# Graph attention on one core: attention and feed-forward woven by clocks, four gather buffers, adjacency lists in quarter rows

## The chip, the cores and the metric

One NeuronCore of one Trainium2 chip runs the whole kernel in one launch. Its engines are TensorE (PE), VectorE (DVE), ScalarE (ACT), GpSimd (POOL) and SyncE (SP). The time is device microseconds of the launch. DMAs are issued from SP, ACT and POOL; the indirect ones, which gather or scatter rows by an index list, from POOL alone.

## The reference

Inputs are `x` and `h_target` (4096 x 512, float32), an adjacency matrix `adj` (4096 x 4096, int32, about 0.4% ones: both directions of a random mask of density 0.00195, and the diagonal), a node mask of ones, and the weights of one transformer layer with eight heads of 64.

```python
hs, ht = layer_norm(x), layer_norm(h_target)
q, k, v = (ht @ Wq + bq) / 8, hs @ Wk + bk, hs @ Wv + bv
logits  = where(adj != 0, q . k, -1e30)          # per head, 4096 x 4096
ctx     = softmax(logits) @ v
ht      = layer_norm(ht + ctx @ Wo + bo)
out     = layer_norm(x + ht + gelu(ht @ W1) @ W2)   # W1: 512 x 2048
```

## The kernel before

Since a row of `adj` has some 8 to 40 ones, the kernel doesn't build the 4096 x 4096 logits. For every target row it makes a list of its neighbours, sorts rows by the length of the list, and for each tile of 128 rows gathers neighbour rows of keys and values, one neighbour ("slot") per row at a time. A tile runs as many slots as its longest row has neighbours; these caps are constants (`CAPS_A`, `CAPS_B`, 600 slots in all over 32 tiles). A general path stands behind a flag and isn't taken.

Stage one. `source_group` normalises 512 rows of `x` and writes their keys and values to a table `kvd` in DRAM (one row of 1024 floats per node). `target_group` does the same for queries, with the residual beside them, into the tables `tqd` (part 0 for the first 20 tiles of rows, part 1 for the other 12). `edges(i)` makes the lists of 128 rows: it loads the adjacency row by halves (2048 columns), ACT takes the sign and counts, DVE multiplies by column numbers within segments of 128 and takes the 8 largest of every segment (`max`), and then five rounds of `max` and `match_replace` merge 256 candidates into 40. Part 0's lists run beside all eight source groups and five target groups. `sort(0)` ranks the 20 tiles' rows by list length and scatters their records with 20 indirect DMAs.

Stage two: the remaining three target groups, nine of the 36 list steps of part 1, and the attention of pair 0.

Stage three. Tiles are handled in pairs; the caps are paired so that pairs hold 35 to 38 slots, but for pair 0 (23), pair 1 (53) and pair 10 (50). `attend(i)` takes four slots at a time: four gathers from POOL into one buffer `kv` (pool `kp`, L734), DVE multiplies the keys by the q row (L781) and reduces per head (L784), ACT takes exp (L787), DVE multiplies the values by it (L768), and PE adds the values up by transposing them into one PSUM tile (L772). A batch's values are done behind the next batch's keys. At the end of a tile the sums are inverted, spread by transposes, and Wo is applied (L814); the addition that gives `h` (L816) is followed by `front(i + 2)`, which requests a later tile's q rows. At the end of a pair, `h` is normalised (POOL's power L584, ACT L834), transposed (PE L843) and becomes `h2T`. `feed(g)` is the feed-forward of a pair: hidden layer (L864), gelu (L867), output layer (L874), last normalisation, and an indirect DMA to the output (L907).

The order is written by weaving generators. `_weave` before takes streams with a number of steps and always advances the one that has done the smallest share of its steps; it is called once per pair, with that pair's attention, the feed-forward of the pair before, and up to eight list steps (three make one tile of lists; so part 1's lists end beside pair 4, and `sort(1)` follows them). The framework takes this order as a priority; its scheduler places instructions on each engine's queue, allocates buffers and writes all waits. On the chip every queue runs in its order.

When stage two is over, its pools are closed and W1 and W2 are loaded into their place.

Of the kernel before, what the change touches and what calls it, by code (L numbers as in the profile page):

```python
# [8 lines left out]
F32 = mybir.dt.float32  # L9
I32 = mybir.dt.int32  # L10
# [382 lines left out]
def _weave(*streams):  # L393

    live = [[g, n, 0] for g, n in streams]
    while live:
        s = min(live, key=lambda s: s[2] / s[1])
        s[2] += 1
        if next(s[0], StopIteration) is StopIteration:
            live.remove(s)  # L400


def _take(gen, n):

    for _ in range(n):
        if next(gen, StopIteration) is StopIteration:
            return
        yield
# [3 lines left out]
def adj_resnorm_kernel(  # L412
# [43 lines left out]
    HW = N // 2  # L456
    SEG = N // P
    SH = SEG // 2
# [28 lines left out]
    with tc.tile_pool(name="keep", bufs=1) as keep:  # L487
# [14 lines left out]
        with ExitStack() as late:  # L502
            lp = late.enter_context(tc.tile_pool(name="lists", bufs=1))
            kp = late.enter_context(tc.tile_pool(name="kv", bufs=3))
# [12 lines left out]
            for i, v in enumerate((ln1_scale, ln1_bias, ln2_scale, ln2_bias, bv)):  # L517
# [6 lines left out]
            dpart = lp.tile([P, NT, 2], F32, name="dpart")  # L524
            cnt = lp.tile([P, NT], F32, name="cnt")
            segoff = lp.tile([P, SEG, 8], F32, name="segoff")
            iota_i = lp.tile([P, SEG, 8], I32, name="iota_i")
            nc.gpsimd.iota(iota_i, pattern=[[P, SEG], [0, 8]], base=0, channel_multiplier=0)
            nc.vector.tensor_copy(segoff, iota_i)
            lio = lp.tile([P, P], BF16, name="lio")  # L530
            nc.gpsimd.iota(iota_i.rearrange("p s e -> p (s e)")[:, :P], pattern=[[1, P]], base=1,
                           channel_multiplier=0)
            nc.vector.tensor_copy(lio, iota_i.rearrange("p s e -> p (s e)")[:, :P])
# [60 lines left out]
            def edges(i):  # L594

                cand = lp.tile([P, SEG, 8], F32, name="cand", bufs=2)
                for h in range(2):
                    a = lp.tile([P, HW], I32, name="a", bufs=2)
                    nc.sync.dma_start(a, adj[i * P:(i + 1) * P, h * HW:(h + 1) * HW])
# [3 lines left out]
                    nc.vector.tensor_tensor(sg, sg, lio.unsqueeze(1).to_broadcast([P, SH, P]),  # L603
                                            ALU.mult)
                    for s in range(SH):
                        nc.vector.max(cand[:, h * SH + s, :], sg[:, s, :])  # L606
                    yield
                gid = lp.tile([P, SEG, 8], F32, name="gid")
                nc.vector.scalar_tensor_tensor(gid, cand, 0.0, segoff, op0=ALU.is_gt, op1=ALU.mult)
# [10 lines left out]
                yield  # L620
# [5 lines left out]
            def sort(part):  # L626
# [13 lines left out]
                oh = pool.tile([P, SH, P], BF16, name="sg", bufs=2)  # L640
# [4 lines left out]
                pos = pool.tile([P, HW], I32, name="a", bufs=2).bitcast(F32)  # L645
# [20 lines left out]
                for i in range(n):  # L666
                    ins = nc.gpsimd.indirect_dma_start(
                        out=recs_d[part][:, :],
                        out_offset=bass.IndirectOffsetOnAxis(ap=ranki[:, i:i + 1], axis=0),
                        in_=R[:, i0 + i, :], in_offset=None)  # L670

                    tc.declare_no_dep(ins.ins, group=f"scatter{part}", reason="other rows")
                    tc.add_to_no_dep_group(f"scatter{part}", ins.ins)

# [22 lines left out]
            def source_group(g, t=None):  # L697
                _, hT = normed(x, g, t)
                yield
                for j in range(G):  # L700
                    kvr = ip.tile([P, 2 * D], F32, name="row")
                    for half, w in enumerate((wk, wv)):
                        pkv = psi.tile([P, D], F32, name="pq")
                        for kc in range(KC):
                            nc.tensor.matmul(pkv, hT[:, kc, j * P:(j + 1) * P], w[:, kc, :],  # L705
                                             start=kc == 0, stop=kc == KC - 1)
                        nc.scalar.copy(kvr[:, half * D:(half + 1) * D], pkv)  # L707
                    r0 = 1 + (g * G + j) * P
                    nc.scalar.dma_start(kvd[r0:r0 + P, :], kvr)
                    yield  # L710

            def target_group(g):
                t, hT = normed(h_target, g)
                yield
                for j in range(G):
# [12 lines left out]
                    yield  # L728


            recs, tqs = {}, {}
# [6 lines left out]
            def prefetch(i):  # L738
# [3 lines left out]
                part = 1 if r0 >= PARTS[1][0] * P else 0  # L742
                r0 -= PARTS[part][0] * P
# [12 lines left out]
            def attend(i):  # L756

                rec, tq, cap = recs[i], tqs[i], TILES[i][1]
                nc.vector.tensor_copy(degs[:, i:i + 1], rec[:, MAXE:MAXE + 1])
                has = sp.tile([P, MAXE], F32, name="has", bufs=1)  # L760
                nc.vector.tensor_scalar(has[:, :cap], rec[:, :cap], 0.0, None, op0=ALU.is_gt)
# [14 lines left out]
                for j0 in range(0, cap, S):  # L776
# [14 lines left out]
                    yield  # L791
                values(*pend.pop(0))
                pm = sp.tile([P, MAXE, H], F32, name="pm", bufs=1)
# [17 lines left out]
                yield  # L811
# [5 lines left out]
                yield h  # L817

            def attend_group(g, res):
                mv = sp.tile([P, T2, 2], F32, name="mv2")  # L820
                hs = []
                for j in range(T2):
                    i = g * T2 + j
                    if i + 3 not in recs:
                        prefetch(i + 3)
                    for r in attend(i):
                        if r is not None:
                            hs.append(r)
                            front(i + 2)
                            stats(sp, r, mv[:, j, :], "n2")  # L830
                        yield
# [4 lines left out]
                yield  # L836
# [12 lines left out]
                res.append(h2T)  # L849

            def att_steps(g):
                return sum(-(-TILES[g * T2 + j][1] // S) + 2 for j in range(T2)) + 2


            def feed(g, h2T):
# [22 lines left out]
                yield  # L878
                for f2 in range(1, FC // 2):
                    now = hidden(f2)  # L880
                    yield
# [15 lines left out]
                    yield  # L897
# [14 lines left out]
            FEED = FC + 1  # L912


            ed = all_edges()
            NA, NBT = PARTS[0][1], PARTS[1][1]
            first = 3 * NA
            work = [source_group(0, first_x)]
            for _ in range(2):
                next(work[0])  # L920
# [3 lines left out]
            order = work + src[:2]  # L924
# [3 lines left out]
            per = 5  # L928
            def chain(gens):
                for g in gens:  # L930
                    yield from g
            _weave((chain(order), per * len(order) - 2), (_take(ed, first), first))
# [3 lines left out]
            for i in range(2):  # L936
                front(i)
            res = []
            qb = chain([target_group(g) for g in range(NA // G, NG)])
            left = 3 * NBT  # L940
            w0 = 9
            _weave((qb, per * (NG - NA // G)), (attend_group(0, res), att_steps(0)),
                   (_take(ed, w0), w0))
            left -= w0
# [10 lines left out]
            for g in range(1, NT // T2):  # L955
                before = res.pop()
                streams = [(attend_group(g, res), att_steps(g)), (feed(g - 1, before), FEED)]
                if left > 0:
                    n = min(left, 8)
                    streams.append((_take(ed, n), n))  # L960
                    left -= n
                    if left == 0:
                        def end_lists(g0=streams.pop()[0]):
                            yield from g0
                            sort(1)
                        streams.append((end_lists(), n))
                _weave(*streams)
            for _ in feed(NT // T2 - 1, res.pop()):
                pass
# [57 lines left out]
```

## Time and profile before

| | |
|---|---|
| median of 3 runs | 2280.63 us (2275.54 to 2283.97) |
| the profiled execution | 2282.18 us, its span 2280.3 us, mean granted clock of TensorE 0.899 |
| busy, us and share of the span | PE 1832.5 (80%), DVE 1670.0 (73%), POOL 1119.4 (49%), ACT 706.2 (31%) |
| gathers of key/value rows | 600 on POOL, 775.1 us busy |
| DMA | 482.28 MB, mean 211 GB/s |

The span is the time from the first to the last instruction; the rest of the execution's time lies around it. Matmuls are pipelined, and their ends are modelled, so PE's busy share is no measure of a peak. The granted clock is a share of 2.4 GHz. POOL's spans are rough. A wait is put down to the releaser that came last.

### The profile page before, as it was taken

To read this page: it belongs to the slowest core of one execution; us is meant where nothing else is said; L and a number is where in the kernel's file an instruction comes from. 1 tells how busy PE (TensorE), PEld (TensorE's weight loads), DVE (VectorE), ACT (ScalarE), POOL (GpSimd) and SP (SyncE) were. 2 spreads that over 40 slices of the span, in tenths; PEclk is the share of its full clock that TensorE was granted. 3 is DMA by queue.
4 is the path that set the end of the run, shared out by engine and by line. 5 is a ranking of instruction groups with operands and counts; after the bars stand their busy time and mean duration, and the time that the engine had idled before them with its cause. 6 is when DMAs were issued, how large, how long until landed. Compare 5 with 4: busy or idle time off the path is not lost. (4 is left out here: it accounts for less than half of the span.)

```text
span 2280.3 us, 20645 instructions
## 1 busy us (share of the span) xinstructions
PE 1832.5 (80%) x7154; PEld 1187.8 (52%) x7154; DVE 1670.0 (73%) x2898; ACT 706.2 (31%) x962; POOL 1119.4 (49%) x887
## 2 busy tenths in 40 slices
PE   6988888457866877686779797978878898878897
PEld 3444434234544555454547565556646566655564
DVE  6998895678788888977476766768686777757540
ACT  4554453202313332231213222323313332322220
POOL 0022222777546463555555546655656556554510
PEclk9999999767877999797989898989999999989898
DMA  8766653668767566565466566666666666655520
GB/s 315 247 238 235 225 207 138 245 228 325 277 215 279 196 226 223 169 238 176 150 215 207 182 240 198 229 212 211 227 229 231 206 229 226 232 165 197 194 65 11
DMA packets 135947, 482.28 MB, mean 211 GB/s; under 512 B 19044, under 2 KB 19608, under 8 KB 127640
## 3 DMA queue, kind: packets, MB, share of 16 engines
q0 software_dynamic: 101760, 365.74, 46.9%
q1 hardware_dynamic: 28368, 96.24, 12.4%
q10 hardware_dynamic: 5704, 18.89, 2.1%
q8 instruction: 58, 0.95, 0.2%
q14 instruction: 57, 0.47, 0.1%
HBM read 438.07 MB, written 42.73 MB: 211 GB/s over the span
## 5 line engine op out<-in xcount | busy, mean ns | idle before, releaser
L734 POOL DMA_INDIRECT kv<-kvd,rec x600 | 775.1, 1292 | 535.6 <-PE cps L772 294.3
L781 DVE TENSOR_TENSOR kv<-kv,tq 128x2048 f32<-128x2048 f32 (+3 forms) x160 | 345.6, 2162 | 340.8 <-DMA kv<-kvd,rec 325.5
L772 PE MATMUL cps<-ident,kv 128*128 128x128 f32 x2400 | 344.4, 303 | 212.8 <-DVE kv L768 212.8
L864 PE MATMUL pf<-h2T,w 128*128 128x256 f32 x2048 | 494.2, 394 | 10.6 <-DMA w<-in_L_gnn_W_dram 5.7
L874 PE MATMUL po<-w,gt 128*128 128x512 f32 x1024 | 469.7, 598 | 4.8 <-ACT gt L867 4.8
L772 PEld LDWEIGHTS cps<-ident,kv 128*128 128x128 f32 x2400 | 313.0, 158 | 283.9 <-DVE kv L768 250.6
L864 PEld LDWEIGHTS pf<-h2T,w 128*128 128x128 f32 x2048 | 396.8, 199 | 99.2 <-issue 36.9
L768 DVE TENSOR_TENSOR kv<-kv,p 128x2048 f32<-128x2048 f32 (+3 forms) x160 | 343.5, 2153 | 27.1 <-ACT p L787 27.0
L784 DVE TENSOR_REDUCE lg<-kv 128x32 f32<-128x2048 f32 (+3 forms) x160 | 342.5, 2143 | 1.2
L874 PEld LDWEIGHTS po<-w,gt 128*128 128x128 f32 x1024 | 191.0, 193 | 190.0 <-issue 181.3
L787 ACT ACTIVATE p<-lg 128x32 f32<-128x32 f32 (+3 forms) x160 | 36.4, 227 | 671.5 <-DVE lg L784 671.0
L606 DVE MAX8 cand<-sg 128x8 f32<-128x128 bf16 x1024 | 227.5, 277 | 0.3
L867 ACT ACT_TABLE_LOAD x97 | 124.5, 1283 | 218.9 <-PE pf L864 218.1
L584 POOL TENSOR_TENSOR n_rs<-n_ve,mhalf 128x2 f32<-128x2 f32 (+1 forms) x48 | 50.2, 1046 | 268.9 <-DVE n_ve L583 263.1
L601 ACT ACTIVATE sg<-a 128x2048 bf16<-128x2048 int32 x64 | 122.1, 1908 | 144.5 <-DVE cand L606 110.4
L814 PE MATMUL m<-wo,ct 128*128 128x512 f32 x256 | 133.9, 672 | 31.4 <-DVE ct L810 31.2
L718 PE MATMUL pq<-wq,hT 128*128 128x512 f32 x256 | 125.8, 641 | 15.0 <-DVE row L721 15.0
L787 ACT ACT_TABLE_LOAD x96 | 123.2, 1283 | 1.7
L867 ACT ACTIVATE gt<-pf 128x512 f32<-128x512 f32 x128 | 76.1, 597 | 152.0 <-PE pf L864 151.0
L705 PE MATMUL pq<-wk,hT 128*128 128x512 f32 x256 | 120.8, 609 | 2.0 <-ACT row L707 2.0
L705 PE MATMUL pq<-wv,hT 128*128 128x512 f32 x256 | 117.0, 597 | 1.2 <-ACT row L707 1.1
L814 PEld LDWEIGHTS m<-wo,ct 128*128 128x128 f32 x256 | 53.2, 215 | 101.4 <-issue 58.3
(112 smaller groups left out, 1453.2 us busy)
## 6 DMA issues: line engine op xcount, KB each, us to landing
a<-in_adj_dram SPq DMA_DIRECT2D x64, 1024.0 KB, 6.0
kvd<-row ACTq DMA_DIRECT2D x32, 512.0 KB, 4.5
tq<-row POOLq DMA_DIRECT2D x32, 512.0 KB, 6.4
kv<-kvd,rec POOLq DMA_INDIRECT x600, 5.9
xin<-in_L_gnn_h_target_dram SPq DMA_DIRECT2D x8, 1024.0 KB, 5.7
w<-in_L_gnn_W_dram SPq DMA_DIRECT2D x8, 1024.0 KB, 20.4
xin<-in_x_dram SPq DMA_DIRECT2D x7, 1024.0 KB, 10.1
xin<-in_x_dram SPq DMA_DIRECT2D x4, 256.0 KB, 2.9
```

The lines of the kernel that those rows point to most:

```text
L606: nc.vector.max(cand[:, h * SH + s, :], sg[:, s, :])
L705: nc.tensor.matmul(pkv, hT[:, kc, j * P:(j + 1) * P], w[:, kc, :], start=kc == 0, stop=kc == KC - 1)
L734: nc.gpsimd.indirect_dma_start(out=dst, out_offset=None, in_=table[:, :], in_offset=bass.IndirectOffsetOnAxis(ap=idx, axis=0))
L768: nc.vector.tensor_tensor(v4, v4, p[:, j0:j0 + n, :].unsqueeze(3) .to_broadcast([P, n, H, HD]), ALU.mult)
L772: nc.tensor.matmul(cps[:, c, :], kv[:, j, D + c * P:D + (c + 1) * P], ident, is_transpose=True, start=j0 + j == 0 and c == 0, stop=j0 + j ...
L781: nc.vector.tensor_tensor(kv[:, :n, :D], kv[:, :n, :D], tq[:, :D].unsqueeze(1).to_broadcast([P, n, D]), ALU.mult)
L784: nc.vector.tensor_reduce(lg[:, :n, :], kv[:, :n, :D].rearrange("p j (h d) -> p j h d", h=H), AX.X, ALU.add)
L787: nc.scalar.activation(p[:, j0:j0 + n, :], lg[:, :n, :], AF.Exp)
L814: nc.tensor.matmul(pa, ct[:, c, :], wo[:, c, :], start=c == 0, stop=c == KC - 1)
L864: nc.tensor.matmul(pf[:, k, :], w1[:, kc, f * P:(f + 1) * P], h2T[:, kc, :], start=kc == 0, stop=kc == KC - 1)
L867: nc.scalar.activation(gt, pf, AF.Gelu_apprx_tanh)
L874: nc.tensor.matmul(po[j], gt[:, k, j * P:(j + 1) * P], w2[:, f, :], start=False, stop=f == FC - 1, skip_group_check=True)
```

## The change

- `_weave` now keeps a clock per stream: each step yields its cost, and the stream with the lowest clock goes next. A stream that yields `None` sleeps until another one has stepped.
- Stage three is one weave instead of fifteen: `attention(1..15)` from clock 0, all feed-forwards in a chain from clock `LEAD` = 12, and part 1's lists with their costs times 2.4. Attention and feed-forward of a pair are both scaled to 60 units. Normalised rows are turned (`turn`, the transposes to `h2T`) two steps into the next pair's attention, and `feed(g)` sleeps until its `h2T` is there. One list comes to 39.8 units, so ten lists end beside pair 7.
- In stage one, lists (332 units) and projections (382 units) start together.
- Key/value buffers go from three to four. Adjacency rows are handled in quarters (1024 columns): `a` keeps two buffers of half the size, `sg` gets three of half the size, and two constants shrink.
- `front(i + 1)` is called after a tile's second batch, in place of `front(i + 2)` at the tile's end.
- For part 1 (12 tiles) the residual's multiplication and addition go from POOL to DVE and the table row is written from SP.
- Two small operations (`degs`, `has`) move from the start of a tile to its end.

```diff
 def _weave(*streams):
-    live = [[g, n, 0] for g, n in streams]
+    live = [[t, n, g] for n, (g, t) in enumerate(streams)]
+    asleep = []
     while live:
-        s = min(live, key=lambda s: s[2] / s[1])
-        s[2] += 1
-        if next(s[0], StopIteration) is StopIteration:
+        s = min(live)
+        cost = next(s[2], StopIteration)
+        if cost is None:
+            asleep.append(s)
             live.remove(s)
+            continue
+        if cost is StopIteration:
+            live.remove(s)
+        else:
+            s[0] += cost
+        for w in asleep:
+            w[0] = max(w[0], s[0])
+        live += asleep
+        asleep = []
...
-            kp = late.enter_context(tc.tile_pool(name="kv", bufs=3))
+            kp = late.enter_context(tc.tile_pool(name="kv", bufs=4))
...
-                for h in range(2):
-                    a = lp.tile([P, HW], I32, name="a", bufs=2)
-                    sg = lp.tile([P, SH, P], BF16, name="sg", bufs=2)
+                for h in range(NQ):
+                    a = lp.tile([P, QW], I32, name="a", bufs=2)
+                    sg = lp.tile([P, SQ, P], BF16, name="sg", bufs=3)
...
-                    nc.gpsimd.tensor_mul(tq[:, D:], t[:, j, :], s1b)
-                    nc.gpsimd.tensor_add(tq[:, D:], tq[:, D:], bob)
                     part = 1 if g * G >= PARTS[1][0] else 0
+                    eng, dma = (nc.vector, nc.sync) if part else (nc.gpsimd, nc.gpsimd)
+                    eng.tensor_mul(tq[:, D:], t[:, j, :], s1b)
+                    eng.tensor_add(tq[:, D:], tq[:, D:], bob)
...
-                    nc.gpsimd.dma_start(tqd[part][r0:r0 + P, :], tq)
+                    dma.dma_start(tqd[part][r0:r0 + P, :], tq)
...
                     if len(pend) > 1:
                         values(*pend.pop(0))
-                    yield
+                    yield 1.8 * n
+                    if j0 == S:
+                        front(i + 1)
...
-                            front(i + 2)
...
+            def attention(groups):
+                for g in groups:
+                    wait = 0
+                    slots = sum(TILES[g * T2 + j][1] for j in range(T2))
+                    for cost in scaled(attend_group(g), 1.8 * slots + 12.0):
+                        yield cost
+                        wait += 1
+                        if later and wait == LAG:
+                            turn(*later.pop())
+                if groups[-1] == NT // T2 - 1 or groups[-1] == 0:
+                    turn(*later.pop())
+                    yield 1.0
...
-            _weave((chain(order), per * len(order) - 2), (_take(ed, first), first))
+            _weave((chain(order), 0), (_take(ed, NA * steps), 0))
             sort(0)
             for i in range(3):
                 prefetch(i)
-            for i in range(2):
-                front(i)
+            front(0)
...
-            _weave((qb, per * (NG - NA // G)), (attend_group(0, res), att_steps(0)),
-                   (_take(ed, w0), w0))
+            _weave((qb, 0), (attention([0]), 5), (_take(ed, first_lists), 10))
...
+            def other_lists():
+                for cost in ed:
+                    yield 2.4 * cost
+                sort(1)
+                yield 1.0
+
+            _weave((attention(range(1, NT // T2)), 0),
+                   (chain(scaled(feed(g), 54.8) for g in range(NT // T2)), LEAD),
+                   (other_lists(), 0))
```

## Rows read from the trace of the kernel before

**Rows 1.** Busy time by stretch: us, each engine's busy us (instructions), clock, DMA share, GB/s

```profile
0.00:393.00 393.00, 338.25 (x895) 158.57 (x896) 324.89 (x1211) 194.70 (x257) 86.47 (x92) 0.95 0.66 231
393.00:537.00 144.00, 83.19 (x258) 45.98 (x256) 105.36 (x218) 31.99 (x44) 107.52 (x90) 0.73 0.69 245
537.00:1065.00 528.00, 389.89 (x1612) 273.61 (x1611) 441.61 (x742) 148.24 (x201) 275.55 (x205) 0.85 0.66 231
537.00:1394.00 857.00, 656.58 (x2751) 460.36 (x2750) 661.21 (x950) 232.03 (x319) 456.95 (x352) 0.87 0.63 218
1394.00:2203.00 809.00, 693.85 (x3037) 483.75 (x3038) 569.79 (x501) 239.63 (x331) 460.89 (x347) 0.94 0.62 207
2203.00:2281.00 78.00, 60.64 (x217) 39.17 (x215) 8.79 (x21) 7.82 (x14) 7.52 (x8) 0.91 0.07 22
```

**Rows 2.** Waits, 537 to 2203 us: who for whom, us, times, longest

```profile
DVE kv L781 <- DMA kv<-kvd,rec: 311.1, 69, 16.1
POOL kv L734 <- PE cps L772: 291.4, 56, 13.2
...
PE t L843 <- ACT h L834: 68.6, 23, 12.0
...
POOL tq L734 <- DVE h L816: 60.9, 14, 9.7
```

**Rows 3.** Timeline of PE: start, us, instructions merged, idle before and its releaser

```profile
643.29 3.67 PE L772 MATMUL cps<-ident,kv 128*128 128x128 f32 x16 [7.24 <-DVE kv L768]
...
1411.57 3.62 PE L864 MATMUL pf<-h2T,w 128*128 128x256 f32 x16
1415.03 1.91 PE L772 MATMUL cps<-ident,kv 128*128 128x128 f32 x16
1416.78 3.60 PE L874 MATMUL po<-w,gt 128*128 128x512 f32 x8
```

**Rows 4.** Timeline of DVE and POOL, gathers beside a product and beside a reduction

```profile
589.46 2.29 DVE L781 TENSOR_TENSOR kv<-kv,tq 128x2048 f32<-128x2048 f32 x1 [8.33 <-DMA kv<-kvd,rec]
589.75 2.82 POOL L734 DMA_INDIRECT kv<-kvd,rec  x1 [0.30 <-issue]
...
2152.62 2.29 DVE L784 TENSOR_REDUCE lg<-kv 128x32 f32<-128x2048 f32 x1
2153.71 0.94 POOL L734 DMA_INDIRECT kv<-kvd,rec  x1 [0.30 <-issue]
```

**Rows 5.** Timeline of ACT: the normalisations that end pairs 14 and 15

```profile
2115.94 1.52 ACT L834 ACTIVATE h<-h,n_nm,n_rs 128x512 f32<-128x512 f32 x2 [4.88 <-DVE n_nm L585]
2202.49 1.52 ACT L834 ACTIVATE h<-h,n_nm,n_rs 128x512 f32<-128x512 f32 x2 [4.46 <-DVE n_nm L585]
```

**Rows 6.** Groups by line, the lists: busy us, mean ns, idle before

```profile
L606 DVE MAX8 cand<-sg 128x8 f32<-128x128 bf16 x1024 | 227.5, 277 | 0.3
...
L603 DVE TENSOR_TENSOR sg<-sg,lio 128x2048 bf16<-128x2048 bf16 x64 | 80.1, 1251 | 4.3 <-ACT sg L601 4.3
```

**Rows 7.** The residual's multiplication on POOL, by line; a 128x512 product on DVE

```profile
L723 POOL TENSOR_TENSOR row<-xin,s1b 128x512 f32<-128x512 f32 x32 | 44.0, 1376 | 97.4 <-issue 35.1 <-DMA kvd<-row 27.2 <-DMA tq<-row 20.4
...
2188.97 0.69 DVE L768 TENSOR_TENSOR kv<-kv,p 128x512 f32<-128x512 f32 x1 [0.93 <-ACT p L787]
```

**Rows 8.** Waits of DVE, 0 to 537 us; timelines of DVE and POOL around the sort

```profile
DVE row L721 <- DMA tq<-row: 24.6, 5, 15.5
...
392.57 1.15 DVE L653 TENSOR_TENSOR_SCAN a<-one_c,t 128x480 f32<-128x480 f32 x1 [15.69 <-PE t L652]
...
401.24 1.10 POOL L667 DMA_INDIRECT rec<-R,ranki  x1 [9.74 <-DVE ranki L665]
...
437.31 0.94 POOL L734 DMA_INDIRECT kv<-kvd,rec  x1 [0.30 <-issue]
```

**Rows 9.** DMA issues: KB each, median us from issue to landing

```profile
a<-in_adj_dram SPq DMA_DIRECT2D x64, 1024.0 KB, 6.0
kvd<-row ACTq DMA_DIRECT2D x32, 512.0 KB, 4.5
```

More of the change, by code (lines that the diff above doesn't have):

```diff
@@ L644, in sort @@
                 ohf = oh.rearrange("p b i -> p (b i)")
-                pos = pool.tile([P, HW], I32, name="a", bufs=2).bitcast(F32)
+                pos = pool.tile([P, QW], I32, name="a", bufs=2).bitcast(F32)
                 pos = pos[:, :NB * n].rearrange("p (b i) -> p b i", b=NB)
@@ L742, in prefetch @@
                 part = 1 if r0 >= PARTS[1][0] * P else 0
+                assert part in done
                 r0 -= PARTS[part][0] * P
@@ L825, in attend_group @@
                         prefetch(i + 3)
-                    for r in attend(i):
-                        if r is not None:
-                            hs.append(r)
-                            front(i + 2)
-                            stats(sp, r, mv[:, j, :], "n2")
-                        yield
+                    yield from attend(i, hs)
+                    stats(sp, hs[j], mv[:, j, :], "n2")
                 rs, nm = rstd_of(sp, mv, T2, "n2")
@@ L835, in attend_group, with turn @@
                                          scale=rs[:, j:j + 1])
-                yield
+                later.append((g, hs))
+            def turn(g, hs):
                 h2T = sp.tile([P, KC, T2 * P], F32, name="h2T")
@@ L848, in attend_group, with feed @@
                                              bias=b2c[:, kc:kc + 1], scale=s2c[:, kc:kc + 1])
[L849 to L855, printed above, removed]
+                h2Ts[g] = h2T
+            def feed(g):
+                while g not in h2Ts:
+                    yield None
+                h2T = h2Ts.pop(g)
                 xs = []
@@ L910, in feed, with chain, scaled @@
                         in_=xs[j], in_offset=None)
-            FEED = FC + 1
+            def chain(gens):
+                for g in gens:
+                    yield from g
+            def attention(groups):
[3 more added lines that the diff above has]
+                    for cost in scaled(attend_group(g), 1.8 * slots + 12.0):
+                        yield cost
+                        wait += 1
[4 more added lines that the diff above has]
+                    yield 1.0
+            LAG, LEAD = 2, 12.0
+            UNIT = 60.0
+            def scaled(gen, total):
+                for cost in gen:
+                    yield cost if cost is None else cost * UNIT / total
             ed = all_edges()
             NA, NBT = PARTS[0][1], PARTS[1][1]
-            first = 3 * NA
-            work = [source_group(0, first_x)]
+            steps = NQ + 1
+            source0 = source_group(0, first_x)
             for _ in range(2):
-                next(work[0])
+                next(source0)
             wq, s1b, bob, bq8 = late_constants()
@@ L923, in adj_resnorm_kernel @@
             src = [source_group(g) for g in range(1, NG)]
-            order = work + src[:2]
+            order = [source0] + src[:2]
             rest = src[2:]
@@ L954, in adj_resnorm_kernel @@
                                   W2[q * D:(q + 1) * D, :].rearrange("(c p) n -> p c n", p=P))
[L955 to L969, printed above, removed]
+            def other_lists():
+                n = 0
+                for cost in ed:
+                    yield 2.4 * cost
+                    n += 1
+                sort(1)
+                yield 1.0
+            _weave((attention(range(1, NT // T2)), 0), (chain(scaled(feed(g), 54.8) for g in range(NT // T2)), LEAD),
+                   (other_lists(), 0))
         with tc.tile_pool(name="s3", bufs=1) as sp, \
```

84 lines of the change are left out of this document (41 added, 43 removed).

## The prediction

> **What bounds the kernel now.** I read the busy time by stretch first, because the kernel has four stages with different limits [rows 1]. In the first (0 to 393 us: key/value rows, query rows, 20 neighbour lists) PE is busy 338 us and DVE 325: both near full. In the second (393 to 537: the sort, the last query rows, the first attention pair) nothing is full, and PE has a granted clock of 0.73. The third, attention beside feed-forward, I cut at 1394, where the seventh of its fifteen pairs ends: DVE is busy 661 of 857 us and PE 657, then DVE 570 of 809 and PE 694. The last (78 us) is the final pair's feed-forward alone. So for 1666 us no engine is full, and the reader should look for what they wait for in turn.
>
> The waits of that stretch [rows 2] are a ring: DVE waits 311 us for gathered rows, GpSimd (POOL) waits 291 us before a gather until PE's transposes have read an old buffer, and those transposes wait for DVE. With three buffers the ring is closed tightly. Two smaller waits stand at the seams: q requests wait 60.9 us for the end of a tile (the addition giving h), and PE waits 68.6 us for a pair's normalised rows, with no feed-forward left to do. An idle PE pays twice: after 7.24 us of idleness 16 transposes took 3.67 us, at the 1.2 GHz level; without it 1.91 us, at 2.4 GHz [rows 3]. So the bound is a round trip, not an engine.
>
> **The floors.** Slots are counted from the caps in the code: pairs 1 to 7 hold 276, pairs 8 to 15 hold 301.
> PE: 16 hidden-layer instructions take from 1411.57 to 1415.03, 3.46 us, and a pair has 128 of them, 27.7 us; eight output instructions take 3.60 with the last one's tail, some 3.43 net, and a pair has 64, 27.4 us; 16 transposes (four slots) take 1.75 us net, 0.437 a slot [rows 3]. Pairs 8 to 15 thus need 8 x 55.1 + 301 x 0.437 + 16 x 3.43 (Wo, same shape as the output) = 627 us at the upper clock.
> DVE: 570 us, measured [rows 1].
> POOL: a gather takes 0.94 us while DVE reduces, 1.25 with its gap. One that starts at 589.75, inside DVE's two-input product (589.46 to 591.75), takes 2.82 and ends 0.82 after it [rows 4]. A full batch of four slots is product, reduction, product, 6.9 us of DVE: run without a break it admits three POOL operations (one behind each product, one more beside the reduction). It needs four gathers and about one other (per pair of nine batches two q, two x and two output requests and two powers); DVE's small operations make room for about one. One is left over: 75 batches x 1.25 = 94 us, so 570 + 94 = 664 us. This is the highest floor.
> On this the Trainium skill ("SBUF — State Buffer", section "Who interferes with whom") says that a DVE instruction with two SBUF inputs excludes a GpSimd instruction that reads SBUF for its whole length; rows 4 agree. The same section infers that descriptor generation is not held up by such an operation; rows 4 say otherwise. By that inference the floor of pairs 8 to 15 would be PE's 627 us.
>
> **The change part by part.** The sum is made against the profiled execution's own 2282.18 us: span 2280.3 plus 1.9 around it, 1.5 above the median of the three runs.
>
> *Fourth gather buffer, q request inside the tile, feed-forward one clock behind.* These have one answer: they lengthen the ring by a third and remove both seams. The q request now stands behind a tile's second batch; it waits for the previous tile's h, with third-batch gathers queued behind it, but two batches are in hand then. The last pair's normalising (68.6 us of PE waits in all) gets feed-forward of the pair before as cover. What is late next is POOL against DVE's products.
> Pairs 8 to 15: between 664 us (floor) and 809 (nothing gained). I take the rate of the nearest row, the best pair of before: pair 15 took 2202.49 - 2115.94 = 86.6 us for 35 slots [rows 5], 2.47 us a slot, x 301 = 744 us: **65 us less**. It is a rate that the three-buffer ring already reached where no later attention competed.
> Pairs 1 to 7: ten lists fall here instead of nine, and are spread over seven pairs, not four. A list costs at least (227.5 + 80.1) / 32 = 9.6 us of DVE [rows 6]; demand becomes 661 + 10 = 671 us. DVE's share was 661/857 = 0.77 in all and 442/528 = 0.84 while lists ran [rows 1]; the ends are 0.77 (871 us) and 0.96 (700). I take 0.88, a little above the row with lists because its maxima let gathers pass: 671/0.88 = 762 us, **95 us less**. The second sort still sends 12 scatters through POOL ahead of gathers; that stall is in the share.
>
> *Query rows of part 1 to DVE and the sync queue (SP).* Off POOL go 12 x 2 operations of 1.37 us [rows 7] and 12 writes. On DVE 24 operations of 0.69 us are added (the width of the 128x512 product in rows 7), 16.6 us. What leaves is DVE's wait for its row buffers, 24.6 us in all and 15.5 at once [rows 8]: POOL was inside the 20 scatters that begin at 401.24 and could not drain them. The two nearly cancel. The price is on SP: a row's write waits there for DVE's addition, and the adjacency and input loads behind it wait too; before, 1024 KB of adjacency landed in 6.0 us and 512 KB rows in 4.5 [rows 9]. Two lists, eight quarter loads: 0 to 8 x 4.5 = 36 us if every one were bare. DVE has attention batches of 6.9 us to do meanwhile, so I take 5.
>
> *Lists ahead at the end of stage one.* By the written costs the 20 lists come to 332 units against 382 for the projections, where they ended level before. The sort needs only lists; before, its DVE work waited 15.69 us for PE at 392.57, its scatters began at 401.24 and the first gather at 437.31 [rows 8]. With lists early the sort can lie beside the last projections; the first gather still needs the last key/value row, near 393. Ceiling of the gain 437 - 400 = 37 us; floor a loss of 15, the same wait turned round, if lists served first starve the projections (both engines are nearly full there). I take 25 from the second stage, less the 5 of SP: 144 becomes 124. If DVE isn't quicker through the lists, the gain is nothing.
>
> *Quarter rows.* The same bytes and maxima, twice the loads, signs and products. What they cost beyond their length isn't in the trace for these shapes; from products of 512 and 2048 elements (0.69 and 2.29 us, [rows 4, 7]) a fixed part of (4 x 0.69 - 2.29)/3 = 0.16 us is an estimate. ACT is busy 195 of 393 us [rows 1] and hides its part; without that cover its signs would hold PE's copies back. For DVE two more products in each of 20 lists are 40 x 0.16 = 6 us; the other end, products that don't shrink at all, is 40 x 1.25 [rows 6] = 50. I take 3, as DVE has gaps there: 393 becomes 396.
>
> *The tail* stays: the last pair's feed-forward needs its attention. 78 us.
>
> **Sum:** 396 + 124 + 762 + 744 + 78 + 1.9 = 2106 us, 2104 against the median; I say **2105 us**, 8% faster. Ends of all terms together: 385 + 100 + 700 + 664 + 76 + 2 = 1927 and 443 + 180 + 871 + 809 + 80 + 2 = 2385.
>
> **The rivals.**
> *A. POOL becomes the bound.* Each batch costs two caught gathers (2.82 + 0.30), two free (1.24 each) and one other operation, 9.97 us x 75 = 748 us, and half of the 16 tiles keep a seam of 60.9/14 = 4.4 us [rows 2], 35 us: 783. Lists keep the share of 0.84: 671/0.84 = 799. The second stage gains 10. Sum 396 + 134 + 799 + 783 + 78 + 2 = 2192. For it: rows 4. Against it: POOL's idle time in that stretch is mostly for buffers [rows 2].
> *B. The floors are nearly reached.* 690 for pairs 8 to 15, a share of 0.93 with lists (722), second stage 110: 396 + 110 + 722 + 690 + 78 + 2 = 1998. For it: every wait of rows 2 is one that buffers or a lag remove. Against it: three floors lie within 15% of each other, and queues in fixed order then collide.
> *C. Slower: lists disturb seven pairs instead of four.* If the waits come from DVE and PE standing in each other's order and not from buffers, every pair with lists costs what pairs 1 to 4 cost, 528/166 slots = 3.18 us a slot [rows 1]: 276 x 3.18 = 878 us, 21 more; nothing else moves, 2303 us. It decides if a pair with one and a half lists costs over 3.1 us a slot.
> *D. The change doesn't do what it says.* The fourth buffer stands empty, since POOL's order (powers, output requests, q requests waiting for DVE) holds gathers back whatever is free: 2280 us. For it: waits beside the buffers in rows 2. Against: 291 us are for buffers by name.
>
> **Chances.** The forecast 0.52 (its own range 2050 to 2165), A 0.20, B 0.14, C 0.09, D 0.05. The range 1985 to 2245 holds the forecast, A and B in all but their own edges, and leaves out C and D; the ends of all terms together lie outside it, since they would have to come at once. About 0.5% is what a measurement of this kernel can tell from no change: faster by more 0.86, within it 0.05, slower 0.09.
>
> **What would show it.** In the new trace: DVE's wait for gathers in the third stage falls from 311 to under 180 us, POOL's wait for PE from 291 to under 120; PE's wait for normalised rows is nearly gone; its granted clock there is above 0.95; mean gather time rises, as more fall inside products; pairs 8 to 15 take 85 to 92 us (the 50-slot one over 110); the first gather stands before 425. The prediction is wrong if DVE still waits 250 us for gathers with four buffers, or if pairs 2 to 7 each take over 115 us.

## The result and the profile after

The changed kernel takes 2129.1 us (median of four runs, 2121.7 to 2131.9), the one before 2282.3 beside it: ratio 0.9329, 95% interval [0.9298, 0.936], 6.7% faster. The forecast was 2105. The profiled execution has a span of 2127.5 us and a mean granted clock of TensorE of 0.925.

First the page's busy times, us (share of the span) and instructions:

```profile
PE 1780.9 (84%) x7154; PEld 1147.5 (54%) x7154; DVE 1679.3 (79%) x2986; ACT 737.8 (35%) x1102; POOL 1160.3 (55%) x851
```

DVE's work is nearly the same as before (1670 us); what shrank is its idle time, and PE's busy time (1833 us before), at a higher clock. Then the changed kernel by stretch, with the columns of [rows 1]; the cuts are again the ends of pairs 0, 7 and 15, and pairs 1 to 7 are shown whole and in two:

```profile
0.00:393.00 393.00, 338.46 (x892) 157.22 (x893) 339.65 (x1293) 208.70 (x344) 84.54 (x90) 0.96 0.69 236
393.00:528.00 135.00, 82.21 (x279) 45.36 (x277) 107.30 (x181) 26.90 (x49) 86.54 (x69) 0.81 0.76 272
528.00:963.00 435.00, 359.33 (x1590) 253.30 (x1591) 383.33 (x559) 156.46 (x224) 289.09 (x192) 0.91 0.76 265
963.00:1265.00 302.00, 257.50 (x1160) 176.01 (x1158) 269.57 (x404) 100.69 (x146) 221.24 (x148) 0.95 0.68 232
528.00:1265.00 737.00, 616.84 (x2748) 429.30 (x2748) 652.90 (x963) 257.16 (x370) 510.33 (x339) 0.93 0.72 252
1265.00:2036.00 771.00, 675.70 (x2996) 471.61 (x2996) 570.69 (x530) 236.74 (x327) 471.31 (x346) 0.93 0.65 215
2036.00:2128.00 92.00, 67.68 (x241) 43.96 (x241) 8.81 (x21) 8.30 (x15) 7.54 (x8) 0.89 0.06 18
```

Against [rows 1]: stages one and two together 537 to 528, pairs 1 to 7 857 to 737, pairs 8 to 15 809 to 771, the end 78 to 92. Most of the gain, 120 of 153 us, lies where DVE is now 89% busy (653 of 737). In pairs 8 to 15 the busiest engine is PE, 88%.

The waits between the ends of pairs 0 and 15 (who for whom, us, times, longest), the answer to [rows 2]; a gather is now L754, the keys product L799, the value product L786, the value transposes L790, Wo L837, h L839, the normalisation L854, the turn's transposes L866:

```profile
DVE kv L799 <- DMA kv<-kvd,rec: 155.9, 45, 15.0
...
POOL kv L754 <- PE cps L790: 143.0, 38, 18.8
...
PE m L837 <- DVE ct L833: 61.7, 17, 10.1
...
POOL tq L754 <- DVE h L839: 57.2, 14, 10.8
...
PE cps L790 <- DVE kv L786: 52.3, 21, 10.5
PE t L866 <- ACT h L854: 51.5, 20, 19.5
```

The two waits of the ring halved. The two at the seams fell far less: 60.9 to 57.2 us for q requests, 68.6 to 51.5 for normalised rows. A third, at the end of a tile, grew and is now PE's longest in this stretch: its wait before Wo for the tile's scaled sums. In the kernel before, in the view of [rows 2]:

```profile
PE m L814 <- DVE ct L810: 26.1, 12, 2.9
```

### The profile page after: what moved, and what is told of

It is laid out like the page before. It is cut to its first block, busy times and chain, and to the rows that moved or that the text cites. A ratio compares the mean times of both kernels' runs of the same rounds, so it can differ in the third digit from the quotient of the medians.

```text
span 2127.5 us, 20996 instructions
## 1 busy us (share of the span) xinstructions
PE 1780.9 (84%) x7154; PEld 1147.5 (54%) x7154; DVE 1679.3 (79%) x2986; ACT 737.8 (35%) x1102; POOL 1160.3 (55%) x851
## 5 line engine op out<-in xcount | busy, mean ns | idle before, releaser
L754 POOL DMA_INDIRECT kv<-kvd,rec x600 | 830.1, 1383 | 337.4 <-issue 158.8
L799 DVE TENSOR_TENSOR kv<-kv,tq 128x2048 f32<-128x2048 f32 (+3 forms) x160 | 344.3, 2153 | 187.6 <-DMA kv<-kvd,rec 158.6
L897 PE MATMUL po<-w,gt 128*128 128x512 f32 x1024 | 474.8, 602 | 14.6 <-ACT gt L890 14.6
L887 PE MATMUL pf<-h2T,w 128*128 128x256 f32 x2048 | 481.2, 386 | 5.7 <-ACT h2T L870 4.8
L887 PEld LDWEIGHTS pf<-h2T,w 128*128 128x128 f32 x2048 | 389.8, 194 | 91.8 <-issue 37.1
L790 PE MATMUL cps<-ident,kv 128*128 128x128 f32 x2400 | 310.4, 284 | 73.5 <-DVE kv L786 73.4
L786 DVE TENSOR_TENSOR kv<-kv,p 128x2048 f32<-128x2048 f32 (+3 forms) x160 | 342.9, 2149 | 25.3 <-ACT p L805 25.1
L790 PEld LDWEIGHTS cps<-ident,kv 128*128 128x128 f32 x2400 | 286.1, 147 | 130.9 <-DVE kv L786 95.3
L599 POOL TENSOR_TENSOR n_rs<-n_ve,mhalf 128x2 f32<-128x2 f32 (+1 forms) x48 | 58.4, 1217 | 358.3 <-DVE n_ve L598 345.9
L621 DVE MAX8 cand<-sg 128x8 f32<-128x128 bf16 x1024 | 226.6, 279 | 0.2
L616 ACT ACTIVATE sg<-a 128x1024 bf16<-128x1024 int32 x128 | 135.2, 1056 | 213.9 <-DMA a<-in_adj_dram 97.8
L837 PE MATMUL m<-wo,ct 128*128 128x512 f32 x256 | 140.3, 699 | 73.7 <-DVE ct L833 64.7
L837 PEld LDWEIGHTS m<-wo,ct 128*128 128x128 f32 x256 | 55.2, 225 | 146.6 <-DVE ct L833 75.7
L736 PE MATMUL pq<-wq,hT 128*128 128x512 f32 x256 | 117.9, 608 | 15.4 <-DVE row L739 14.4
```

The source lines that it names most:

```text
L621: nc.vector.max(cand[:, h * SQ + s, :], sg[:, s, :])
L754: nc.gpsimd.indirect_dma_start(out=dst, out_offset=None, in_=table[:, :], in_offset=bass.IndirectOffsetOnAxis(ap=idx, axis=0))
L786: nc.vector.tensor_tensor(v4, v4, p[:, j0:j0 + n, :].unsqueeze(3) .to_broadcast([P, n, H, HD]), ALU.mult)
L790: nc.tensor.matmul(cps[:, c, :], kv[:, j, D + c * P:D + (c + 1) * P], ident, is_transpose=True, start=j0 + j == 0 and c == 0, stop=j0 + j ...
L799: nc.vector.tensor_tensor(kv[:, :n, :D], kv[:, :n, :D], tq[:, :D].unsqueeze(1).to_broadcast([P, n, D]), ALU.mult)
L837: nc.tensor.matmul(pa, ct[:, c, :], wo[:, c, :], start=c == 0, stop=c == KC - 1)
```

## Experiments

In each comparison the kernel before ran on the same chip; its medians were 2273.7 to 2282.3 us, so ratios are compared.

**1 to 3. Buffer or weave?** The two parts that the prediction had priced as one were set against each other, two by two.

```
e1:  -  kp = ...tile_pool(name="kv", bufs=4)      (changed kernel)
     +  kp = ...tile_pool(name="kv", bufs=3)
e5:  the kernel before + quarter-row lists and small constants
e6:  e5, and  kp = ...tile_pool(name="kv", bufs=4)
```

> The changed kernel with three gather buffers instead of four; the weave and the quarter-row lists stay. Theory W (the weave is the gain: PE has feed-forward to do while DVE is at a piece, so a piece no longer stands behind a whole feed-forward): VectorE's wait for gathers between the first pair's end and the last's goes from 156 us to about 200, and the time to 2150 to 2175 us. Theory B (the fourth buffer is the gain: the gather of a piece is issued one piece earlier): that wait goes back to 280 us or more, and the time to 2220 us or more.

> The kernel before with the quarter-row lists and their smaller constants alone; three buffers, the old weave, the old request of q rows. The lists' DVE work keeps its sum (max by 128 columns, one product of the same elements in two halves), so both theories expect no gain in the third stage: 2270 to 2295 us, unless the shorter DVE products by themselves let gathers through (then 2255 or less).

> The kernel before with the quarter-row lists and four gather buffers, under the old weave. Theory W: PE still sits in a whole feed-forward while the pieces pile up behind it, so a buffer more is filled earlier but released as late; 2235 to 2270 us, with VectorE's wait for gathers at 220 us or more. Theory B: most of the gain is there, 2190 us or less, with that wait near 160 us.

Ratios to the kernel before:

| | three buffers | four buffers |
|---|---|---|
| old weave, quarter rows | 1.0003 [0.9974, 1.0031] | 0.9475 [0.9438, 0.9513] |
| changed kernel | 0.9762 [0.9719, 0.9805] | 0.9329 [0.9298, 0.936] |

Theory B's times came, 2223.7 and 2156.5 us: the buffer alone is worth 5.3% under the old weave, 4.3% under the new. The rest of the change gives 2.4% with three buffers, 1.5% with four; quarter rows alone nothing (2276.4 us). By the ends of pairs in the traces, in pairs 8 to 15 the buffer takes 817 to 759 us under the old weave and 792 to 770 under the new: there the rest of the change gains 25 us with three buffers and loses 11 with four. The waits lie between what the theories named. Between the ends of pairs 0 and 15, DVE's wait for gathers with three buffers under the new weave, then with four under the old (L784 is its keys product):

```profile
DVE kv L799 <- DMA kv<-kvd,rec: 234.9, 70, 11.0
```

```profile
DVE kv L784 <- DMA kv<-kvd,rec: 189.3, 48, 9.7
```

And the stretch of pairs 8 to 15 of the latter, in which the old weave is quicker than the new (760 us against 771):

```profile
1320.00:2080.00 760.00, 679.37 (x3033) 471.61 (x3032) 568.28 (x509) 237.79 (x328) 460.20 (x348) 0.95 0.66 218
```

**4. The keys step with one input** (operands shortened).

```
-  nc.vector.tensor_tensor(kv keys, kv keys, tq broadcast, ALU.mult)
+  nc.vector.tensor_reduce(kv keys, kv keys.unsqueeze(3), AX.X, ALU.add)
```

> The changed kernel with the keys product by q replaced by a reduction over an axis of length one of the same shape: the multiplication by q is left out, and the instruction reads one tile instead of two. Theory L (a gather's start on GpSimd is held by a VectorE product of two inputs): the gathers' mean falls from 1.38 to about 1.15 us and those that fall beside the keys step to 0.95, and the time falls by 10 to 40 us if the new step is not longer than the product (2.3 against 2.29 us). Theory N (they are long for another reason, such as the DMA rings): the mean stays within 0.05 us, and the time follows VectorE's busy time alone.

2076.7 us, 0.9129 [0.9087, 0.917]. Groups by line (busy us, mean ns; then idle time before): gathers fell from 1383 ns to 1173, and the new keys step is as long as the product was (2153 ns).

```profile
L754 POOL DMA_INDIRECT kv<-kvd,rec x600 | 704.0, 1173 | 380.2 <-PE cps L790 185.6 <-issue 149.3 <-DVE kv L799 21.6
L799 DVE TENSOR_REDUCE kv<-kv 128x2048 f32<-128x2048 f32 (+3 forms) x160 | 342.8, 2143 | 152.5 <-DMA kv<-kvd,rec 134.7 <-issue 17.5
```

In its timeline a gather inside the one-input step takes 0.95 us and one inside the value product, which still has two inputs, 3.02:

```profile
1650.25 2.29 DVE L799 TENSOR_REDUCE kv<-kv 128x2048 f32<-128x2048 f32 x1
1651.48 0.95 POOL L754 DMA_INDIRECT kv<-kvd,rec  x1 [0.30 <-issue]
...
1655.15 2.29 DVE L786 TENSOR_TENSOR kv<-kv,p 128x2048 f32<-128x2048 f32 x1 [0.30 <-ACT p L804]
1655.24 3.02 POOL L754 DMA_INDIRECT kv<-kvd,rec  x1 [0.30 <-DMA xt<-in_x_dram,rec]
```

Over the whole run, of the 121 gathers that start inside the one-input step none takes more than 1.01 us; in the changed kernel the 90 that start inside the keys product take 2.27 us in the median. The edit also frees the keys step of its wait for q rows, but in the changed kernel DVE waits only 3.1 us for them between the ends of pairs 0 and 15.

Theory L, and more than it asked: 52 us. Pair ends in the trace put 37 of them in pairs 1 to 7 (738 to 701) and 14 in pairs 8 to 15 (770 to 756).

**5. The sort inside the weave.**

```
-  _weave((chain(order), 0), (_take(ed, NA * steps), 0))
-  sort(0)
+  def first_part():
+      yield from _take(ed, NA * steps)
+      sort(0)
+      yield 1.0
+  _weave((chain(order), 0), (first_part(), 0))
```

> The changed kernel with the sort of the first half's lists written inside the weave, behind its last list, and not after it. In the changed kernel the second PE step of that sort stands behind every projection that is left (written at 359, run at 393 us), and the first gather comes at 436.8 us. Theory Q (PE's order holds the sort): the first gather comes 20 to 35 us earlier, and the time falls by 15 to 35 us, to 2095 to 2115. Rival: the last rows of keys and values (their write issued at 397 us) or the second stage's list work hold the first pair, the sort's earlier end buys nothing, and the time is 2120 to 2135.

In the changed kernel the sort's second PE step (L669) waits behind all the projections, though its first ran at 359 us. PE's timeline:

```profile
359.49 0.36 PE L669 MATMUL t<-sg,ones_bf 128*128 128x480 bf16 x1 [0.63 <-DVE sg L659]
...
389.52 3.60 PE L723 MATMUL pq<-wv,hT 128*128 128x512 f32 x8
392.95 0.37 PE L669 MATMUL t<-sg,ones_bf 128*128 128x480 bf16 x1
```

Its first gather on POOL, and that of the kernel with the sort inside:

```profile
436.84 0.96 POOL L754 DMA_INDIRECT kv<-kvd,rec  x1 [0.30 <-issue]
```

```profile
413.89 0.94 POOL L754 DMA_INDIRECT kv<-kvd,rec  x1 [8.83 <-DMA a<-in_adj_dram]
```

So theory Q is right on the cause: 23 us earlier. But 2122.5 us, 0.9285 [0.9239, 0.933], can't be told from the changed kernel: pair 0 ends only 7 us earlier (520.4 against 527.6), pair 7 ends 13 us earlier and pair 15 again only 6. The rival's time is what came; which of its two reasons it is stays open.

**6. The place of the q request.** `front(i + 1)` in the middle of a tile becomes `front(i + 2)` behind `hs.append(h)`, and two requests instead of one stand ahead of pair 0, as before.

> The changed kernel with the q rows of a part requested when the part two before it has its h (two parts ahead), as in the kernel before, and not in the middle of the part before. Theory 1 (the request's place is worth nothing once the weave keeps parts in order): 2120 to 2140 us, with VectorE's wait for q rows within 10 us. Theory 2 (the request at a part's end sits behind gathers on GpSimd's queue and delays the seam): 2145 us or more and longer waits where a part begins.

2116.0 us, 0.9261 [0.9228, 0.9294]: 0.7% faster than the changed kernel, the intervals just apart, and below the ranges of both theories. The wait of POOL for h is 50.0 us against 57.2. The new place buys nothing.

**7. The target rows of the second half.**

```
-  eng, dma = (nc.vector, nc.sync) if part else (nc.gpsimd, nc.gpsimd)
+  eng, dma = nc.gpsimd, nc.gpsimd
```

> The changed kernel with the target rows of the second half assembled on GpSimd with GpSimd's queue, as in the kernel before, and not on VectorE with SyncE's. Theory 1 (GpSimd is the scarcer in pairs 1 to 7, where lists and gathers meet): 10 to 30 us slower, 2140 to 2160. Theory 2 (VectorE is: 88% busy there): VectorE gives up about 8 x 4 row steps, 10 to 20 us faster, 2110 to 2120. Neither: within 8 us.

2108.2 us, 0.9243 [0.9208, 0.9279]: faster, as theory 2 said, but not for its reason. The part has 12 such rows (not 8 x 4), and in the changed kernel their work on DVE stands wholly ahead of the end of pair 0. Its multiplications (count, ns min/median/max, first and last start):

```profile
L744 DVE TENSOR_TENSOR row<-xin,s1b x12: 673/692/693, 393.7 to 512.5; 128x512 f32<-128x512 f32 x12
```

So pairs 1 to 7 have none of it to give up. Those pairs without the edit's rows on DVE, all engines, then the maxima of the lists alone (L621, 32 to a list), there and in the changed kernel:

```profile
543.00:1255.00 712.00, 613.24 (x2748) 428.42 (x2748) 634.83 (x876) 241.28 (x351) 514.42 (x347) 0.94 0.75 259
```

```profile
543.40:1255.00 711.60, 53.99 (x252) 0.94 0.75 259
```

```profile
527.60:1265.00 737.40, 64.61 (x304) 0.93 0.72 252
```

DVE does 18 us less there, since list work (52 maxima with what belongs to them) has moved ahead of pair 0's end, which comes 16 us later (543.4 against 527.6); the stretch is 25 shorter. That leaves 10 us by the end of pair 7. Pairs 8 to 15, which have no lists, take 9 us less, for a reason that no run shows; another 10 are at the very end, told below.

**8. Lists in four pairs.** `yield 2.4 * cost` in the list stream becomes `yield 1.44 * cost`.

> The changed kernel with the second half's lists spread over about four pairs instead of seven. Theory D (pairs 1 to 7 are bound by VectorE's sum, 653 us busy of 738): pairs 1 to 4 lengthen, 5 to 7 shorten by as much, the sum of the seven stays within 12 us of 738 and the time is 2120 to 2145. Theory C (lists beside gathers are what costs, and thinner is better): denser lists make the seven pairs 25 us longer or more, 2150 or more.

2167.6 us, 0.9506 [0.9454, 0.9559]: the time of theory C. Pairs 1 to 4, 5 to 7, 8 to 15:

```profile
529.00:1002.00 473.00, 368.56 (x1594) 257.84 (x1594) 434.33 (x771) 166.80 (x246) 277.98 (x194) 0.88 0.73 255
1002.00:1297.00 295.00, 250.36 (x1126) 174.99 (x1126) 221.30 (x212) 93.15 (x125) 199.04 (x146) 0.94 0.66 217
1297.00:2074.00 777.00, 681.85 (x3026) 474.37 (x3024) 571.84 (x511) 237.31 (x329) 466.55 (x347) 0.94 0.65 214
```

Pairs 1 to 4 take 38 us more than in the changed kernel, at a share of DVE of 0.92, so there D holds. Pairs 5 to 7 give back 7 only, although they shed 48 us of DVE. The second sort falls in pair 5 here and in pair 7 in the changed kernel; pair 6, which has no sort in either, takes 90.3 us without lists and 91.3 with its share of them. Something else than DVE's sum holds that pair, and what it is wasn't tried. The reading that fits: thinly spread lists fill DVE time that this other limit leaves free; packed, they don't.

**9 to 12. The seam.** In the changed kernel PE's timeline around the end of pair 11, with the normalisation at 1662.7:

```profile
1649.47 3.62 PE L887 MATMUL pf<-h2T,w 128*128 128x256 f32 x16
1652.93 1.91 PE L790 MATMUL cps<-ident,kv 128*128 128x128 f32 x16
1654.67 3.60 PE L897 MATMUL po<-w,gt 128*128 128x512 f32 x8
1658.11 1.04 PE L790 MATMUL cps<-ident,kv 128*128 128x128 f32 x8
1663.56 0.33 PE L866 MATMUL t<-ident,h 128*128 128x128 f32 x1 [4.42 <-ACT h L854]
```

The turn's transposes stand next on PE's queue and wait, with transposes of gathered values behind them. So these edits were made to the changed kernel. `LAG` counts the steps of the next pair's attention behind which the turn is written, and `LEAD` is in the weave's clock, 60 units to a pair:

```
e8:    -  LAG, LEAD = 2, 12.0
       +  LAG, LEAD = 4, 24.0
e10:   +  LAG, LEAD = 2, 24.0
e11:   LAG, LEAD = 4, 24.0 and the edits of 5, 6 and 7
e12:   LAG, LEAD = 6, 36.0 and the edits of 5, 6 and 7
```

> The changed kernel with the feed-forward held four pairs behind the attention at most and a lead of 24 us, instead of two and 12. Theory S (what is left of the seam waits is feed-forward that runs out just when a pair ends): PE has more to do at a seam, pairs 8 to 15 shorten by 2 to 4 us each, and the end behind the last pair grows by about 40 to 80 us (one feed-forward is about 37 us of PE's time), so the whole is 2130 to 2180. Rival: the clocks of the weave keep the feed-forward at its place anyway, the bound is never reached, and the time is 2125 to 2135.

> The changed kernel with the feed-forward's clock held back by 24 us instead of 12, and the turn of a pair's rows still behind the second piece of the next pair. It parts the two halves of the run with 4 and 24, which took 2056.8 us. Theory T (the gain there is the turn's place on PE's queue: the transposes that wait for the normalised rows stand ahead of the next pair's transposes, 51 us of PE's wait and gather buffers held meanwhile): with the turn where it was, PE's wait for those rows stays at 45 us or more and the time at 2110 to 2135. Theory F (the gain is the feed-forward's place, PE has work left at the seam): 2055 to 2085 us, whatever that wait is.

> The four single edits that gained, in one kernel: turn behind the fourth piece with a lead of 24, the second half's target rows on GpSimd, the q rows requested two parts ahead, the first half's sort inside the weave. If they act at different places (the turn on PE in all pairs, the rows on VectorE in pairs 1 to 7, the sort ahead of pair 0) they add: 2129 - 72 - 21 - 13 - 6 = 2017 us. If they save the same wait (gather buffers held at a seam) the sum is 2040 or more.

> The same with the turn behind the sixth piece and a lead of 36 us. Theory T: at four pieces PE's wait for the normalised rows is already about 12 us, so two pieces more buy at most that and lengthen the end by about 12 us: within 12 us of the kernel with four. Theory F (more feed-forward left at the seam always helps): 15 us or more below it.

The first of these takes `LAG` for a distance in pairs, which it isn't, and a feed-forward is not 37 us of PE's time but 55.1 by the prediction's sum.

| | us | ratio to before | pairs 1 to 7, 8 to 15 (trace) | PE waits for rows, whole run |
|---|---|---|---|---|
| changed | 2129.1 | 0.9329 [0.9298, 0.936] | 738, 770 | 52.0 |
| e10 | 2075.2 | 0.9114 [0.9074, 0.9155] | 711, 731 | 28.4 |
| e8 | 2056.8 | 0.8999 [0.8963, 0.9035] | 710, 711 | 12.2 |
| e11 | 2047.3 | 0.8978 [0.8927, 0.9029] | 704, 714 | 6.9 |
| e12 | 2090.0 | 0.918 [0.9133, 0.9226] | 707, 739 | 4.6 |

The lead alone is worth 54 us, in theory F's range; the wait for rows fell too, where theory T had it stay at 45 or more. The turn's later place gives 18 more behind the longer lead; without it, it wasn't run. With both, PE works through the same seam (e8, pair 11's normalisation at 1600.3):

```profile
1598.80 3.60 PE L897 MATMUL po<-w,gt 128*128 128x512 f32 x8
1602.24 3.62 PE L887 MATMUL pf<-h2T,w 128*128 128x256 f32 x16
1605.69 1.91 PE L790 MATMUL cps<-ident,kv 128*128 128x128 f32 x16
1607.44 3.60 PE L897 MATMUL po<-w,gt 128*128 128x512 f32 x8
1610.87 0.60 PE L866 MATMUL t<-ident,h 128*128 128x128 f32 x4
```

The other edits don't add to it, the second of e11's two cases: e11 and e8 can't be told apart, and the 10.6 us between their profiled spans lie behind the attention's end (1949.7 and 1949.4). More of both constants is worse: e12, the miss of both theories, loses 25 us in pairs 8 to 15 to e11 and 20 elsewhere. One wait that grew in pairs 8 to 15:

```profile
DVE degs L811 <- DMA rec<-rec: 42.8, 10, 5.7
```

It is 2.5 us in e11. A pair's records stay in their six buffers until its feed-forward has written its output, so a later feed-forward can hold up the next records' loads. But the same wait is 26.6 us in the changed kernel, whose feed-forward is the earliest, and 2.6 in e8: lag alone doesn't set it, and the cause of e12's loss stays open.

## Why the prediction was right, and where its steps failed

**The ring.** That the bound was a round trip through three buffers, and that the fourth would pay, held: 311 to 156 us for DVE, 291 to 143 for POOL. The prediction gave buffer, weave and q request one price and one answer. The runs part them: the buffer is 64 to 79% of the whole gain (4.3 or 5.3 of 6.7%), the q request less than nothing, and the weave as written 1.5 to 2.4% with all its company. Rival D, an empty fourth buffer, is excluded by e1: in the changed kernel itself the buffer is worth 4.3%.

**The sum came closer than its terms.** 2105 against 2129 hides two misses that cancel by luck: pairs 1 to 7 came 25 us under their forecast, pairs 8 to 15 some 26 over. What is left, 8 us ahead of the end of pair 0 and 14 behind the attention, makes the difference.

**Pairs 1 to 7: 762 forecast, 737 measured.** DVE's share of 0.88 was right (653/737 = 0.886); the demand was put 18 us too high, at 671. That DVE is the limit there is shown in part: in e4 18 us less of its list work gave 25, in e7 denser lists cost 38; but pair 6 of e7 takes as long without lists as with them. Rival C did not come about, since at the change's pace a list pair costs 435/166 = 2.62 us a slot for pairs 1 to 4 against its 3.1; e7 shows that the danger in it was real, with 38 us in the same pairs.

**Pairs 8 to 15: 744 forecast, 770 measured.** The step that failed is "remove both seams": PE still waits at them. The rate, 2.47 us a slot, was read from the last pair [rows 5], the one behind which no attention stands, and the others didn't reach it. The last two pair ends of the changed kernel:

```profile
1950.82 1.52 ACT L854 ACTIVATE h<-h,n_nm,n_rs 128x512 f32<-128x512 f32 x2 [5.08 <-DVE n_nm L600]
2035.36 1.52 ACT L854 ACTIVATE h<-h,n_nm,n_rs 128x512 f32<-128x512 f32 x2 [5.75 <-DVE n_nm L600]
```

84.5 us for the last pair, 97.9 for the seven before it, which is 2.58 us a slot. With a lead of 12 too little feed-forward stands ahead of the turn on PE's queue: in pairs 8 to 15 PE waits 41 us for normalised rows and 48 for a tile's sums. With a lead of 24 and the later turn (e8) these are 2 and 24, PE's clock there is 0.96 in place of 0.93, and the stretch takes 711, under the forecast. The rate taken was reachable, but not by the change as written.

**The highest floor was not the limit.** More gathers were caught by products, as forecast: 178 of 600 take over 1.3 us, 143 before, and the mean rose from 1292 to 1383 ns. Rival A's 783 us for pairs 8 to 15 lie nearer to the 770 than the forecast's 744, but not by its mechanism: 79 gathers are caught there, about one a batch and not two, POOL is busy 471 of 771 us, and e9, which frees half of the catches, saves only 14 us there. PE, busy 676, with its waits at the seams makes up most of that stretch. Where DVE is full the catches cost more, 37 us. On the Trainium skill's inference ("SBUF — State Buffer", section "Who interferes with whom") that descriptor generation is not held by a two-input DVE operation, e9 decides against it for these gathers: 0.95 us beside one input, 3.02 beside two of the same length, in one kernel. PE's floor of 627 us left out 24 small transposes a pair, some 21 us at the 0.109 of [rows 3]; in e8 PE is busy 653 in that stretch, at a clock of 0.96.

**The second stage: 124 forecast, 135 measured.** "With lists early the sort can lie beside the last projections" failed at PE's order, not at DVE: the sort was written behind the projections and its second step ran behind them. The first gather stayed at 437 (437.31 in [rows 8]). Where it came 23 us earlier (e2), pair 0 ended at 520.4, the 396 + 124 of the forecast: the term was about right for an order of PE's queue that the change didn't write. In the whole time of e2 the gain is too small to tell.

**Query rows to DVE: called nearly even, in fact a loss.** e4 gains 0.9% by undoing it. The DVE wait that it was to remove did go (24.6 us [rows 8] to 6.1; 23.1 in e4), and pair 0 ends 16 us earlier with it. The operations' own time on DVE falls there too, as forecast; what the prediction left out is that list work is then placed behind pair 0's end, 18 us of DVE in pairs 1 to 7, and that the span's end grows by 10.

**The tail: 78 forecast, 92 measured.** From the last normalisation to the end of the last output request it takes 77 us against 72, as more feed-forward is left over (241 PE instructions behind the attention, 217 before [rows 1]). The other 9 follow the last request.

Of the signs named beforehand, DVE's wait, the gathers' length and the 50-slot pair (117.5 us) came; POOL's wait (143, not under 120), PE's wait for rows, the clock (0.93, not over 0.95) and the first gather did not, and of the other seven pairs from 8 on four took 95 to 99 us, not 85 to 92.

## What to carry to other kernels

Price a buffer and a schedule apart, and run them apart: here, with a ring of waits that named buffers on both sides, the buffer was the larger part. When two streams share PE, look at what stands on its queue where one stream waits for a result: enough of the other must be left to run ahead of it, and two constants of the weave were worth 72 us beside the 153 of the whole change. When work moves to another engine, look in both traces where it stands and what has moved around it: here pair 0 ended 16 us earlier, and list work went into the fuller stretch behind it.

## What the runs showed of the hardware that was not expected

The span ends 15 us after the last output request wherever the second half's query rows are written through SP's queue, and some 5.4 where they go through GpSimd's. The last request of the changed kernel (span 2127.5) and of e4 (span 2098.9):

```profile
2111.43 0.97 POOL L930 DMA_INDIRECT out_dram<-xt,rec  x1 [2.81 <-issue]
```

```profile
2092.57 0.97 POOL L930 DMA_INDIRECT out_dram<-xt,rec  x1 [2.93 <-issue]
```

15.1 and 5.4 us. The gap is 14.9 to 15.1 in all eight kernels of the first kind and 5.3 to 5.7 in all six of the second, the kernel before among them. No engine is busy in it, but POOL's own instruction queue (POOLq) is, with two instructions at the program's end. The changed kernel, then e4 (count, ns min/median/max, first and last start):

```profile
L1026 POOLq INC_SWDGE_SEM  x1: 2435/2435/2435, 2115.0 to 2115.0; - x1
L1054 POOLq DRAIN  x3: 44/107/9220, 2117.5 to 2127.3; - x3
```

```profile
L1026 POOLq INC_SWDGE_SEM  x1: 560/560/560, 2095.9 to 2095.9; - x1
L1054 POOLq DRAIN  x3: 44/107/1543, 2096.5 to 2098.6; - x3
```

They are 1.9 and 7.7 us longer, nearly the whole difference, and all fourteen kernels have the one pair of times or the other (2.44 and 9.22 us, or 0.56 and 1.54). Why the queue of those rows' writes sets them stays open.
